# Cross-attention over 32 images: the last two groups of context products spread through the pipeline's fill

## The chip, the cores and the metric

One core of one Trainium2 chip. A core has five engines that run side by side, each with its own queue in program order: TensorE (PE: matmuls, with its weight loads PEld), VectorE (DVE), ScalarE (ACT), GpSimd (POOL) and SyncE (SP), which here only issues DMAs. They wait for one another by semaphores. The metric is the device time of one execution in microseconds (us), as the median of several.

## The reference

```python
q = heads(x @ to_q_w)                                  # x (32, 512, 640), 20 heads of 32
txt = ctx[:, :77]                                      # ctx (32, 77, 1024); the other three parts are empty
p = softmax(q @ heads(txt @ to_k_w).T / sqrt(32))
out = merge(p @ heads(txt @ to_v_w)) @ to_out_w + to_out_b + x
```

The context has 77 rows per image, so the three further attentions of the reference have no keys and add nothing. All is float32, and the kernel keeps that accuracy by splitting each matmul operand into a high and a low part and taking three products (high x high, high x low, low x high).

## The kernel before

**Context first.** The 32 x 77 = 2464 context rows are taken in five groups of up to 512 (`GROUPS_KV`; the last, `LAST` = 4, has 416). For each group the context is loaded (`load_context`), transposed on VectorE in eight pieces (`transpose_context`, line 164), split (`split_context`: high part on ScalarE, low part on VectorE), and multiplied by the key and the value weights: five chunks j of 128 channels, eight pieces k, three matmuls each (`context_product`, line 186). One such step of three matmuls is what the tables call a token. A finished key chunk is split and stored to `k_dram` (`split_keys`, two buffers `ks`), a finished value chunk is turned on VectorE, split and stored to `v_dram` (`split_values`, two buffers `vs`). The loops of lines 362 to 414 do this: the values of group g, with the next group's context in between, then the keys of group g + 1. The weights are split on the way in the first group (`first`, line 311). While group 3's values are made, x of image 0 is loaded by SP (line 391), then transposed on VectorE (line 404) and split, high part on ScalarE and low part on POOL. The keys of group 4 follow in two rounds. Only its values are left over.

**Attention by pairs.** Image b and chunk c of 128 channels (four heads) make a pair n = 5 b + c, 160 in all. A pair passes through these steps, spread over some five pairs' time: query product (15 matmuls, five tokens), its split (high on ScalarE, halves copied on POOL, low on VectorE), four score tiles (three matmuls each, into three PSUM banks), row maximum on VectorE, four exponentials per tile on ScalarE, sums, division on POOL, a block transpose on VectorE, a store to DRAM and a load back with keys on the partitions (`pd`, `raw`), a split of that (`pp`), six value matmuls (`pa`), the two halves added, a split (`at`), and, per image, 40 projection tokens (`po`) with output weights `wo_s`, residual and bias, and the store.

**The order is written out by hand.** A table of tokens gives the program order, and so each engine's queue: `FILL` (line 733) for images 0 and 1, `PLAN` (line 771) for each image from 2 to 30, and `LAST_` for the end. A token with a or b in front belongs to image 0 or 1, its digit is the chunk (b5 is chunk 0 of image 2, pair 10), and the letter is the step: q query, Q, k, g its split, s score tile, m maximum, e exponentials, r and N sums and division, z block transpose, w store, d load, c, R, l its split, v value product, A and a halves, h and L split, p projection, f, o, b output, T, X, x transpose and split of the next image's x, u the loads (uk keys, uv values, ux x, ur residual). Tokens with Y are special ones of the fill (`special`, line 900): YC value product of the last group, YT, YH, YL, YD its turning, split and store by POOL's queue, Yk key loads, Yx the load of image 1's x, Yq, YQ, Yc, Yg pair 0's query, Ym the memsets of `vb`, Yw the output weights, Yb the bias. Only the order inside one engine's queue counts; between engines the semaphores decide.

**Memory.** Buffers stand in pools that are opened and released at places in this order, and a tile in reused memory waits for the last use of what was there. Before the table starts, the pools of the context (`kvw`, `kvc`, `kvt`, and the eight banks `psk`) are released and `main` and `ps` opened; `open_late` (line 725) releases `kvp` and the three banks `psv` when the first rows are loaded (token a3d0), and the first Yw releases `kva`.

Of the kernel before, what the change touches and what calls it, by code (L numbers as in the profile page):

```python
# [24 lines left out]
Q = 32  # L25
# [26 lines left out]
def kernel(  # L52
# [83 lines left out]
    kvt = tc.alloc_tile_pool(name="kvt", bufs=2, side="right")  # L136
# [8 lines left out]
    wk_s = kvt.tile([P, NK, 2, C], FPR, name="wk_s", bufs=1)  # L145
    GROUPS_KV = [(g0, min(G, NT - g0)) for g0 in range(0, NT, G)]
    cts, pks, pvs, css, craws, wraws = ({} for _ in range(6))
# [16 lines left out]
    def transpose_context(g, k):  # L164
        gn = GROUPS_KV[g][1]
        craws[k] = kvt.tile([P, G], F32, tag="craw", name="craw")
        nc.vector.transpose(
            craws[k][:, :gn].rearrange("p (a j) -> p a j", j=Q),
            css[g][0][:, : gn // Q, k * Q : (k + 1) * Q],
        )  # L170

    def split_context(g, k):
        gn = GROUPS_KV[g][1]
        ct = kvp.tile([P, 2, G], FPR, tag="ct", name="ct", bufs=9)
        split(ct[:, 0, :gn], ct[:, 1, :gn], craws.pop(k)[:, :gn])
        cts[g, k] = ct
# [22 lines left out]
    def keys(g, j, k):  # L199
        context_product(pks, "pk", g, j, k, wk_s[:, :, :, j * P : (j + 1) * P], psk)  # L200
# [5 lines left out]

    def split_keys(g, j):
        g0, gn = GROUPS_KV[g]
        ks = kvt.tile([P, 2, G], FPR, tag="ks", name="ks")
        split(ks[:, 0, :gn], ks[:, 1, :gn], pks.pop(j)[:, :gn])  # L210
        engine = nc.gpsimd if g + 1 < len(GROUPS_KV) else nc.sync if j < 3 else nc.scalar
        j0 = GROUPS[GROUP_OF[j]][0]
        engine.dma_start(
            k_dram[GROUP_OF[j]][:, :, j - j0, g0 : g0 + gn].bitcast(F32), ks[:, :, :gn].bitcast(F32)
        )
# [6 lines left out]
    def value_parts(j):  # L222
        vs, na = vss[j % 2], GROUPS_KV[LAST][1] // Q
        return vs[:, :na, 0], vs[:, :na, 2], vs[:, :na, 2].bitcast(F32)

    def turn_values(j):
        na = GROUPS_KV[LAST][1] // Q
        nc.vector.transpose(
            value_parts(j)[2], pvs.pop(j)[:, : na * Q].rearrange("p (a d) -> p a d", d=HD)
        )  # L230

    def high_values(j):
        hi, lo, vt = value_parts(j)
        nc.scalar.copy(hi, vt)

    def low_values(j):
        hi, lo, vt = value_parts(j)
        nc.vector.tensor_tensor(lo, vt, hi.bitcast(F32), ALU.subtract)

    def store_values(j, i):  # L240
        g0, gn = GROUPS_KV[LAST]
        dst = v_dram[g0 : g0 + gn, :, j].rearrange("(a t) i c d -> i t a (c d)", t=Q)
        nc.gpsimd.dma_start(  # L243
# [4 lines left out]
    def split_values(g, j, between=None):  # L248

        g0, gn = GROUPS_KV[g]  # L250
        na = gn // Q
        vs = vss[j % 2]
        vt = vs[:, :na, 2].bitcast(F32)
        nc.vector.transpose(vt, pvs.pop(j)[:, :gn].rearrange("p (a d) -> p a d", d=HD))
        if between is not None:
            between()
        split(vs[:, :na, 0], vs[:, :na, 2], vt)
        dst = v_dram[g0 : g0 + gn, :, j].rearrange("(a t) i c d -> i t a (c d)", t=Q)
        for i in range(HPC):
            nc.sync.dma_start(  # L260
                dst[i].bitcast(F32),
                vs[i * Q : (i + 1) * Q, :na].rearrange("p a c d -> p a (c d)").bitcast(F32),
            )

    xts, xss, xpool = {}, {}, []

    def load_x(b, quarters=range(4)):
# [5 lines left out]
        for q in quarters:  # L273
            nc.sync.dma_start(xs[q * Q : (q + 1) * Q, :, :], src[q])
# [10 lines left out]
    def high_x(b, c, high=nc.scalar.copy):  # L285
        xts[b, c] = xpool[0].tile([P, 2, S], FPR, tag="xt", name="xt", bufs=7)
# [18 lines left out]
    zero = kvt.tile([P, 2, G], FPR, name="zero", tag="ks")[:, 0]  # L305
# [5 lines left out]
    def first(*ks):  # L311
# [3 lines left out]
        for k in ks:  # L315
            split_context(0, k)
            split_weights(wk_s[:, k], wk, k)
# [44 lines left out]
    for g in range(LAST):  # L362
        for j in range(NC_):
# [13 lines left out]
            if j == NC_ - 1:  # L377
# [3 lines left out]
                split_values(g, 3, (None, split_wq, split_wo, None)[g])  # L381
                context(g + 1, *range(3, NK))
                if g + 1 == LAST:
                    kvw.release()
                    kvc.release()
# [639 lines left out]
```

## Time and profile before

| | |
|---|---|
| median of the runs | 1873.78 us (1872.28 to 1873.96) |
| profiled execution | 1872.94 us, its span 1871.1 us |
| TensorE busy, weight loads | 1852.1 us, 1660.1 us |
| VectorE, ScalarE, POOL busy | 1559.3, 1525.0, 1298.7 us |
| values of group 3 start | 200.4 us |
| keys of group 4 start | 227.6 us |
| `FILL` starts | 250.0 us |
| first score tile of pair 0, 5, 10 | 265.6, 310.0, 360.5 us |

A row of a stretch of the span gives each engine's busy time in it with its number of instructions, the clock granted to TensorE as a share of full speed, the busy share of the DMA engines, and GB/s. A row of a group gives line, engine, operation, the tiles, the count, busy us and mean ns of one, and the idle time before it with what ended it. In a row in order of time the first number is the start, the second the length, and a bracket says how long the engine had been idle and what released it.

### The profile page before, as it was taken

To read this page: it belongs to the slowest core of one execution; us is meant where nothing else is said; L and a number is where in the kernel's file an instruction comes from. 1 tells how busy PE (TensorE), PEld (TensorE's weight loads), DVE (VectorE), ACT (ScalarE), POOL (GpSimd) and SP (SyncE) were. 2 spreads that over 40 slices of the span, in tenths; PEclk is the share of its full clock that TensorE was granted. 3 is DMA by queue.
4 is the path that set the end of the run, shared out by engine and by line. 5 is a ranking of instruction groups with operands and counts; after the bars stand their busy time and mean duration, and the time that the engine had idled before them with its cause. 6 is when DMAs were issued, how large, how long until landed. Compare 5 with 4: busy or idle time off the path is not lost.

```text
span 1871.1 us, 37477 instructions
## 1 busy us (share of the span) xinstructions
PE 1852.1 (99%) x10332; PEld 1660.1 (89%) x10332; DVE 1559.3 (83%) x2494; ACT 1525.0 (82%) x6210; POOL 1298.7 (69%) x1116
## 2 busy tenths in 40 slices
PE   9999998999999999999999999999999999999998
PEld 7888897899999999999999999999999999999998
DVE  5445347999999999999999999999999999999996
ACT  3233228999999999999999999999999999999984
POOL 1100057888877877777787778877788778877774
PEclk9999999999999999999999999999999999999999
DMA  9878879999998999999899999999989989999985
GB/s 183 200 196 245 199 166 254 233 245 238 242 239 234 240 232 237 238 231 245 237 238 238 237 242 238 238 233 236 241 232 245 240 236 240 229 241 236 238 222 185
DMA packets 565023, 431.37 MB, mean 231 GB/s; under 512 B 191120, under 2 KB 473168, under 8 KB 564816
## 3 DMA queue, kind: packets, MB, share of 16 engines
q1 hardware_dynamic: 559760, 413.62, 86.6%
q0 software_dynamic: 4416, 14.34, 2.3%
q8 instruction: 85, 1.39, 0.3%
q14 instruction: 122, 1.00, 0.2%
q10 hardware_dynamic: 640, 1.02, 0.2%
HBM read 247.17 MB, written 181.64 MB: 229 GB/s over the span
## 4 chain that ended last, share of the span: by engine, by line
PE 81%; ACT 1%; DVE 1%; DMA 1%; issue 0%; POOL 0%; SPq 0%; DVEq 0%; POOLq 0%; ACTq 0%
PE po L685 30%; PE pq L481 28%; PE pa L632 12%; PE sc L516 11%; ACT pn L541 1%; DMA pd<-z 0%; DMA raw<-pd 0%; DVE qt L723 0%; ACT pp L601 0%; DVE z L562 0%; SPq L571 0%; DVE xs L278 0%; POOL v_dram L243 0%; PE pv L191 0%; DVE nm L527 0%
## 5 line engine op out<-in xcount | busy, mean ns | idle before, releaser
L541 ACT ACTIVATE pn<-sc,nm 128x77 f32<-128x77 f32 x2560 | 795.7, 342 | 37.3 <-DVE nm L527 33.8
L685 PE MATMUL po<-wo_s,at 128*128 128x320 f32 x3840 | 710.8, 311 | 0.4 <-DVE at L667 0.2
L685 PEld LDWEIGHTS po<-wo_s,at 128*128 128x128 f32 x3840 | 620.7, 189 | 42.9 <-DVE xr L700 0.6
L481 PE MATMUL pq<-xt,wq_s 128*128 128x512 f32 x2400 | 599.1, 395 | 4.5 <-DVE qt L723 4.5
L541 ACT ACTIVATION_READ_ACCUMULATOR pn<-sc,nm 128x1 f32 x2560 | 567.1, 222 | 0.0
L481 PEld LDWEIGHTS pq<-xt,wq_s 128*128 128x128 f32 x2400 | 436.8, 188 | 86.2 <-ACT pn L541 3.9
L556 POOL TENSOR_TENSOR pn<-pn,rs 128x1232 f32<-128x1232 f32 x160 | 387.0, 2419 | 88.9 <-DVE rs L551 87.0
L632 PE MATMUL pa<-pp,vb 128*128 128x512 f32 x960 | 343.1, 406 | 2.9 <-DVE at L667 1.4
L516 PEld LDWEIGHTS sc<-kb,qt 128*128 128x128 f32 x1920 | 305.4, 189 | 20.7 <-ACT pn L541 6.1
L527 DVE TENSOR_REDUCE nm<-sc 128x4 f32<-128x308 f32 x640 | 294.9, 466 | 22.8 <-PE sc L516 17.1
L516 PE MATMUL sc<-kb,qt 128*128 128x154 f32 (+1 forms) x1920 | 304.2, 275 | 3.8 <-ACT pn L541 2.6
L719 POOL CAST qt<-qt 64x512 fp32r<-64x512 f32 x320 | 195.1, 610 | 139.0 <-ACT qt L715 122.2
L650 DVE TENSOR_TENSOR pa<-pa,aw 64x512 f32<-64x512 f32 x320 | 222.2, 694 | 51.4 <-ACT aw L646 44.2
L617 POOL TENSOR_TENSOR pp<-raw,pp 64x512 fp32r<-64x512 f32 x160 | 206.2, 1289 | 73.2 <-ACT pp L599 58.2
L562 DVE STREAM_TRANSPOSE z<-pn 128x1280 f32<-128x1280 f32 x160 | 241.1, 1507 | 6.1 <-POOL pn L556 2.4
L646 ACT COPY aw<-pa 64x1024 f32<-64x1024 f32 x160 | 161.9, 1012 | 91.9 <-PE pa L632 91.0
L723 DVE TENSOR_TENSOR qt<-pq,qt 64x512 fp32r<-64x512 f32 x320 | 216.8, 677 | 17.6 <-ACT qt L715 12.9
L292 POOL TENSOR_TENSOR xt<-xs,xt 128x512 fp32r<-128x512 f32 x160 | 204.0, 1302 | 35.8 <-ACT xt L288 30.9
L678 POOL TENSOR_TENSOR xr<-xr,bias 128x640 f32<-128x640 f32 x128 | 204.2, 1596 | 12.7 <-issue 2.8
L610 DVE TENSOR_TENSOR pp<-raw,pp 128x1024 fp32r<-128x1024 f32 x160 | 194.3, 1214 | 0.0
L632 PEld LDWEIGHTS pa<-pp,vb 128*128 128x128 f32 x960 | 174.4, 190 | 13.0 <-DVE pp L610 1.6
L601 ACT CAST pp<-raw 128x1024 fp32r<-128x1024 f32 x160 | 168.0, 1050 | 0.8 <-DMA v_dram<-vs 0.8
(48 smaller groups left out, 1577.7 us busy)
## 6 DMA issues: line engine op xcount, KB each, us to landing
pd<-z SPq DMA_DIRECT2D x640, 160.0 KB, 3.5
raw<-pd SPq DMA_DIRECT2D x160, 512.0 KB, 4.4
xs<-in_x_dram SPq DMA_DIRECT2D x128, 320.0 KB, 5.7
xr<-in_x_dram SPq DMA_DIRECT2D x128, 320.0 KB, 3.9
out_dram<-xr SPq DMA_DIRECT2D x127, 320.0 KB, 3.8
raw<-pd SPq DMA_DIRECT2D x160, 128.0 KB, 3.9
v_dram<-vs SPq DMA_DIRECT2D x80, 192.0 KB, 4.1
k_dram<-ks POOLq DMA_DIRECT2D x20, 512.0 KB, 4.3
```

The source lines that it names most:

```text
L481: nc.tensor.matmul(pqs[n], wq_s[:, k, a, j * P : (j + 1) * P], xts[b, k][:, c, :], start=(k == 0 and m == 0), stop=(k == NC_ - 1 and m == 2),)
L516: nc.tensor.matmul(sc[:, cols], qt[:, m, t * P : (t + 1) * P], keys_, start=(m == 0), stop=(m == 2),)
L527: nc.vector.tensor_reduce(nm, sc[:, :KCOLS].rearrange("p (h k) -> p h k", k=NKEY), AX.X, ALU.max, negate=True)
L541: nc.scalar.activation(pnb[n % 2][:, at, :NKEY], sc[:, i * NKEY : (i + 1) * NKEY], AF.Exp, bias=nm[:, i : i + 1], accum_out=sms[n][:, at : ...
L556: nc.gpsimd.tensor_tensor(pf, pf, rs.unsqueeze(2).to_broadcast([P, NQ * HPC, NKEY]), ALU.mult)
L562: nc.vector.transpose(z.rearrange("p b t j -> p t b j"), pn.rearrange("p (t h) k -> p t (h k)", t=NQ).rearrange("p t (b i) -> p t b i", i=Q),)
L617: nc.gpsimd.tensor_tensor(pp[64:, 4, :], raw[:64, 2, :], pp[:64, 4, :].bitcast(F32), ALU.subtract)
L632: nc.tensor.matmul(pas[n][:, p, :], vb[:, p, t, :], pp[:, c, :], start=(c == p), stop=(c == p + 2),)
L650: nc.vector.tensor_tensor(pa[64 * p : 64 * p + 64, 0], pa[:64, p], aw[:, p], ALU.add)
L678: nc.gpsimd.tensor_tensor(xrs[b, t], xrs[b, t], bias, ALU.add)
L685: nc.tensor.matmul(pos[b, t, h][:, :HALF], ats[b * NC_ + j][:, a, t * P : (t + 1) * P], wos[0][:, j, c, h * HALF : (h + 1) * HALF], start= ...
L723: nc.vector.tensor_tensor(qt[rows, 1 + w, :], pqs[n][rows], qt[rows, 0, :].bitcast(F32), ALU.subtract)
```

## The change

- `FILL` begins one group earlier. The values of group 3 (YV, turned Yt, split Yh and Yl, stored Ys by SP), the context of group 4 (Yr transpose, Yf high, Yd low part), x of image 0 (Yz load by POOL's queue, Ya transpose, YU high, Yu low part), the keys of group 4 (YJ, split YI and Yi, stored Yo by SP) and its values (YC) are tokens of one table now. The loops end with group 2's values and group 3's keys. All 160 pairs have the same steps as before; `PLAN` and `LAST_` are as they were.
- The last YC stands at pair 5 (between b0R and b0h), where it stood at the end of pair 2 (before a3s0).
- The key weights `wk_s` are two tiles (384 and 256 columns) in two pools, each split by its own instructions.
- The buffers of the attention are opened in five steps: `open_small` (kb0 and the small tiles, where the context was), `open_first` (qt, pn, over the first key weights), `open_second` (kb1, z, vb, over the second), `open_values` (raw, pp, aw, one at, over the first value weights) and `open_late` (the other at, bias, xr, wo_s, over the rest). The banks are opened by `open_banks` at the first YJ: four for scores and query, two and two for the context products. The memsets of kb and pn are tokens (Yn, Yp).
- The split parts of x stand in two pools of 4 and 3, and the eight `at` buffers are fixed tiles used in turn.

```diff
-    wk_s = kvt.tile([P, NK, 2, C], FPR, name="wk_s", bufs=1)
+    wk_s = [
+        pool.tile([P, NK, 2, c1 - c0], FPR, name=f"wk_s{i}")
+        for i, (pool, (c0, c1)) in enumerate(zip((kvt, kvu), WV))
+    ]
...
-            split_weights(wk_s[:, k], wk, k)
+            part = wraws.pop((id(wk), k))
+            for (c0, c1), dst in zip(WV, wk_s):
+                split(dst[:, k, 0], dst[:, k, 1], part[:, c0:c1])
...
-    for g in range(LAST):
+    for g in range(LAST - 1):
...
-                    load_x(0)
...
-    for i in range(NQ):
-        transpose_x(0, i)
-    for c in range(NC_):
-        split_x(0, c)
-
-    for round_ in (range(3), range(3, NC_)):
-        for k in range(NK):
-            for j in round_:
-                keys(LAST, j, k)
-        for j in round_:
-            split_keys(LAST, j)
...
+    def open_banks():
+        nonlocal ps, psa, psb
+        if ps is None:
+            psk.release()
+            ps = ctx.enter_context(
+                tc.tile_pool(name="ps", bufs=1, space=PSUM, side="right", reuse_waits="tile")
+            )
+            psb = tc.alloc_tile_pool(name="psb", bufs=2, space=PSUM, side="right", reuse_waits="tile")
+            psa = tc.alloc_tile_pool(name="psa", bufs=2, space=PSUM, reuse_waits="tile")
...
+    def open_first():
+        if not qts:
+            open_small()
+            kvt.release()
+            pool = ctx.enter_context(tc.tile_pool(name="first", bufs=1, reuse_waits="tile"))
+            qts.extend(pool.tile([P, 3, S], FPR, name=f"qt{n}") for n in range(2))
+            pnb.extend(pool.tile([P, NQ * HPC, KPAD], F32, name=f"pn{n}") for n in range(2))
...
+        "YV00 YV10 YV20 YV11 YV30 YV31 YV01 YV12 YV02 YV13 YV32 YV03 YV04 YV05 YV14 Yr0 YV06 Yf0 Yz1 Yd0 "
+        "YV07 Yz2 YV15 Yt0 YV40 Yz0 Yr1 Yz3 YV21 Yr2 Yf1 YV41 Yh0 YV42 Yf2 YV33 Yd2 Yr3 YV22 Yl0 YV23 "
+        "Yf3 Yd1 Ys00 YV16 Yr4 Ys01 YV24 Ya1 Ys02 YV43 Ya2 YV34 Ys03 Yf4 Yd3 YV35 Yr5 Yd4 YV25 Ya3 YV17 "
+        "YV44 Yt1 YV26 Ya0 Yf5 YV36 YU0 YV27 Yh1 YV45 YU1 Yt2 YV46 YU2 Yd5 YU3 Yl1 YV37 Yu2 Yr6 Yh2 Ys11 "
+        "YV47 Yf6 Yl2 Ys13 Yu1 Yr7 Ys10 Yd6 Yf7 Ys21 Ys22 Ys23 Ys12 Yt3 Yd7 YU4 Yu4 Yu3 Yu0 Yx0 Ys20 Yx2 "
+        "Yx1 Yh3 Yn0 Yt4 YJ00 YJ01 YJ20 YJ21 YJ10 YJ02 YJ22 YJ30 YJ11 YJ03 YJ12 YJ13 YJ23 YJ14 YJ24 YJ15 "
+        "YJ04 YJ05 YJ06 YJ16 YJ25 YJ31 YJ07 YJ32 YI0 YJ17 Yi0 Yq0 Yl3 YI1 Yo0 Yh4 YJ26 Yi1 YJ40 Yl4 Yo1 "
+        "YJ27 Yx3 YJ41 Yq1 YI2 Yq2 Yi2 YJ42 Yo2 Yq3 Ys41 YJ33 Ys43 Yq4 a1T1 YJ43 Ys30 YQ YJ44 Yg1 Yc1 "
+        "Yk030 YJ45 Yg0 Yc0 Yk000 YJ34 Yk020 a0T0 YJ46 Yp1 Yk010 YJ35 Yk031 YJ36 Yk001 Yp0 Yk021 YJ37 "
+        "Yk011 YJ47 YI3 a0K00 YC00 Yi3 YI4 a0K01 a0q0 Yi4 Yo3 a0q1 Yo4 Yn1 YC01 Ys40 Ym0 a0s0 a0q2 Ys42 "
...
+        "b2g1 b2A b2uv05 b2s3 b3uk011 b2m2 b3q0 b3c0 b2uv01 b2m3 b2a0 b2e1 b3q1 b2uv02 b2k0 b2a1 b3q2 "
+        "b3d1 b1K10 b2e2 b2uv06 b2z b2b0 b3s0 b3uk031 b3q3 b3h b3q4 b3L b3l Yw3 b3c1 b3p1 b3m0 b2w1 b3p4 "
...
+        elif op == "V":
+            values_of_chunk(LAST - 1, *arg, psk)
...
+        elif op == "z":
+            load_x(0, arg, nc.gpsimd)
...
+        elif op == "J":
+            open_banks()
+            keys(LAST, *arg, bank_of("k", arg[0]))
```

300 lines of the change are left out of this document (185 added, 115 removed), and 66 rows, old and new, of the table FILL.

## The prediction

> **What bounds the kernel now.** I read the page's engine lines first, then the stretches of the span by stage, then TensorE's waits and its order of time where it waits.
>
> ```profile
> PE 1852.1 (99%) x10332; PEld 1660.1 (89%) x10332; DVE 1559.3 (83%) x2494; ACT 1525.0 (82%) x6210; POOL 1298.7 (69%) x1116
> ```
>
> ```profile
> 0.00:8.10 8.10, 4.65 (x13) 3.39 (x13) 1.86 (x4) 2.53 (x3) 6.96 (x14) 1.00 0.95 139
> 8.10:200.40 192.30, 192.30 (x841) 158.68 (x842) 91.74 (x144) 58.69 (x101) 11.37 (x17) 0.99 0.90 210
> 200.40:265.60 65.20, 64.09 (x311) 57.74 (x310) 24.80 (x40) 14.77 (x27) 19.31 (x21) 1.00 0.66 166
> 265.60:310.00 44.40, 41.62 (x220) 36.96 (x218) 30.25 (x51) 32.08 (x162) 34.60 (x41) 1.00 0.91 238
> 310.00:360.50 50.50, 44.19 (x208) 35.41 (x208) 45.27 (x71) 48.13 (x197) 38.69 (x32) 0.93 0.94 248
> 360.50:1800.00 1439.50, 1439.50 (x8343) 1307.11 (x8342) 1315.20 (x2110) 1326.77 (x5577) 1148.50 (x965) 1.00 0.91 237
> 1800.00:1871.10 71.10, 65.79 (x404) 60.79 (x403) 50.20 (x78) 42.08 (x148) 39.27 (x29) 1.00 0.67 204
> ```
>
> The columns are window, length, then busy us of PE, PEld, DVE, ACT and POOL, the granted clock, DMA share, GB/s. From 360.5 to 1800 TensorE never idles: nothing can be won there without less work, and the change leaves that table alone. TensorE idles 3.45 us at the start, 5.3 in the drain, and 1.1 + 2.8 + 6.3 = 10.2 in the three rows from 200.4 to 360.5: there the pipeline fills. In 310:360.5 ScalarE is busy 48.13 of 50.5 us and VectorE 45.27; TensorE has too little to do and waits for them.
>
> ```profile
> PE pq L481 <- DVE qt L723: 4.5, 3, 2.1
> PE sc L516 <- ACT pn L541: 2.6, 3, 2.0
> PE pk L191 <- ACT wk_s L103: 2.0, 1, 2.0
> ```
>
> ```profile
> 320.00:322.00 2.00, 0.33 (x3) 0.33 (x3) 1.86 (x3) 1.98 (x11) 0.42 (x1) 1.00 1.04 238
> 322.00:324.00 2.00, 1.16 (x5) 0.53 (x3) 1.88 (x3) 2.00 (x13) 1.27 (x1) 0.60 0.79 293
> 324.00:326.00 2.00, 2.00 (x8) 1.76 (x9) 2.00 (x4) 2.00 (x14) 0.44 (x1) 0.50 0.95 280
> ```
>
> The waits are for query parts and for score banks. After the 2.0 us wait the granted clock fell to half; the 0.93 of row 310:360.5 is 0.07 x 50.5 = 3.5 us of clock lost.
>
> **The idea in numbers.** Matmul work is conserved, so the change is worth what the fill loses less what the new fill loses. I find where pair 10 (b5), from which TensorE waits no more, makes its first score tile. Today's marks, pairs 0, 3, 5 and 10:
>
> ```profile
> 265.57 0.68 PE L516 MATMUL sc<-kb,qt 128*128 128x308 f32 x3
> 296.90 0.86 PE L516 MATMUL sc<-kb,qt 128*128 128x308 f32 x6
> 310.03 0.60 PE L516 MATMUL sc<-kb,qt 128*128 128x308 f32 x3
> 360.50 0.49 PE L516 MATMUL sc<-kb,qt 128*128 128x308 f32 x3
> ```
>
> Prices for a token: V and the 416-wide J and C from the first two rows below (27.36/40 = 0.684; 14.72/26 = 0.566), q 3.49/5 = 0.70, s 0.69/2 = 0.345, v 0.47/2 = 0.235, p 2.24/5 = 0.45, one e on ScalarE 1.23.
>
> ```profile
> 200.37 27.36 PE L191 MATMUL pv<-ct,wv_s 128*128 128x512 f32 x120
> 227.56 14.72 PE L191 MATMUL pk<-ct,wk_s 128*128 128x416 f32 x78
> 379.05 3.49 PE pq L481 x15
> 378.36 0.69 PE sc L516 x6
> 386.22 0.47 PE pa L632 x2
> 383.31 2.24 PE po L685 x15
> 322.59 1.23 ACT pn L541 x8
> ```
>
> **Key weights in two tiles.** Eight casts of 640 columns become 384 and 256, on ScalarE and VectorE each.
>
> ```profile
> L103 ACT CAST wk_s<-wraw 128x640 fp32r<-128x640 f32 x8 | 5.8, 725 | 3.4 <-DMA wraw<-in_L_xattn_to_k_w_dram 3.4
> L103 ACT CAST wv_s<-wraw 128x384 fp32r<-128x384 f32 x8 | 4.1, 511 | 9.7 <-DMA wraw<-in_L_xattn_to_v_w_dram 9.7
> L103 ACT CAST wv_s<-wraw 128x256 fp32r<-128x256 f32 x8 | 3.2, 401 | 0.0
> ```
>
> The first key matmul waited 2.0 us for that cast; the first piece is 0.21 shorter: -0.2 us (0 if its data decide). The cost, 0.511 + 0.401 - 0.725 = 0.19 us for each of eight steps, lies on an engine busy 58.69 of 192.3 us, and matmuls there never wait: nothing.
>
> **Values of group 3, then its followers (V, r/f/d, x).** V starts at 200.4 as before: everything ahead is the same. Until pair 0's first score the table holds 40 V (27.4), 40 J (22.6), 7 q (4.9) and 2 C (1.1): 56.0 us, so 256.4 without waits. The same count on today's kernel, from 227.56: 40 keys, 13 C, 10 q make 37.0, plus the 1.1 us wait that 200.4:265.6 shows (65.2 less 64.09): 265.7 against 265.57 measured. The attention thus starts 9 us sooner and leaves 38 C steps for later instead of 27.
>
> What must be in time here is on the queues. VectorE is held by the last key split of group 3 until 211.5, 11.1 us into V, and then has 27 transposes and differences of 0.6 to 0.8 us:
>
> ```profile
> 210.82 0.69 DVE L104 TENSOR_TENSOR ks<-pk,ks 128x512 fp32r<-128x512 f32 x1 [2.89 <-ACT ks L103]
> 243.42 6.30 POOL L292 TENSOR_TENSOR xt<-xs,xt 128x512 fp32r<-128x512 f32 x5 [30.93 <-ACT xt L288]
> L167 DVE STREAM_TRANSPOSE craw<-cs 128x416 f32<-128x416 f32 x8 | 4.6, 598 | 0.1
> L278 DVE STREAM_TRANSPOSE xs<-xs 128x640 f32<-128x640 f32 x128 | 104.8, 821 | 7.3 <-DMA xs<-in_x_dram 7.3
> v_dram<-vs SPq DMA_DIRECT2D x20, 192.0 KB, 3.7
> xs<-in_x_dram SPq DMA_DIRECT2D x12, 320.0 KB, 5.8
> k_dram<-ks SPq DMA_DIRECT2D x3, 416.0 KB, 3.4
> kb<-k_dram SPq DMA_DIRECT2D x24, 28.9 KB, 2.6
> k_dram<-ks POOLq DMA_DIRECT2D x20, 512.0 KB, 4.3
> 252.92 8.07 SPq L451 DMA_DIRECT2D kb<-k_dram  x12
> ```
>
> In us from V's start: x leaves by POOL's queue, four issues from +12, and lands (5.8) by about +21. VectorE's list, in its order, then puts x's transposes at +24 and the last context transpose at +29, after which ScalarE makes the last high part of x (YU4), near +30. POOL's last low part (u0) is three of 6.30/5 = 1.26 later, +34. SP has the next batch's x (Yx0) waiting for u0, and behind it the store Ys20; this lands near +39 at 3.7, +42 if it stands behind x. The transpose Yt4 waits for it on VectorE, and behind it stand Yi0, Yl3, Yi1. By the order in which banks come free, Yq0 takes the bank Yt4 empties: due at +41.3; YJ40 needs Yi0's bank at +42.6. So 0 to 2 us of wait; I take 0.7. Next, Yo2 (about +46) lands 3.4 later, and the eight loads behind it take 8.07/12 = 0.67 each and a landing of 2.6: +57, where pair 0's score is due at +56.7: 0 to 2, I take 0.8. The memsets of POOL (kb, pn, vb) are the old ones, moved. The last three (Yn1, Ym0, Ym1) wait for the last J at +53.6 and a key store, and stand on POOL ahead of pair 1's query copies; at about 1.26 us each, the price of a low part of x, the nearest row, they end near +58, while pair 1's query is ready near +60 behind ScalarE's second e: nothing, and 2 us if the key store lands late. The other openings wait for steps long done: the raw tile for YC27, some 3 us of TensorE ahead of its load a3d0, the last buffers for YC47 and the value stores, a pair ahead of their first use. The fixed at tiles and the two pools for x keep the old rotation of 8 and 7: nothing, since TensorE idles nowhere in the part where they rotate, with the same reuse distance as before. The four loads of x leave SP and cost POOL issue time while it only waits; the two key stores of ScalarE's queue go to SP, behind nothing but Yx3. Range of this stage 0 to 4 us; sum: 256.4 - 0.2 + 1.5 = 257.7.
>
> **Pairs 0 to 4.** Between their first score tile and pair 5's the table has 37 C, 23 q, 20 s and 6 v: 20.9 + 16.1 + 6.9 + 1.4 = 45.3; ScalarE has 20 e; today's row 265.6:310, with 19 e, keeps it busy 32.08 us. TensorE binds. Interleaving costs something: today's pairs 0 to 2 count 30.4 and take 31.3 (265.57 to 296.90), so 46.6. Value loads stand on SP behind stores (YD), and a query bank behind VectorE (today 1.1 us): 1.3 (0 to 3). Pair 5 at 305.6, against 310.03.
>
> **Pairs 5 to 9.** Here before and after differ little. TensorE: 29 q, 20 s, 30 v, 13 p, 1 C, in all 40.6, against 24, 20, 33, 14 and none, 37.7 today. ScalarE loses against today one e (1.23), one A and two c1 (1.05 each by the first row below, all 1024 wide) and a c0, and gains a Q and an H of about the size of a c0: some 3.9 less, 44.3. VectorE loses one z (1.51), and two a against a T and an L: 43.7.
>
> ```profile
> L601 ACT CAST pp<-raw 128x1024 fp32r<-128x1024 f32 x160 | 168.0, 1050 | 0.8 <-DMA v_dram<-vs 0.8
> L562 DVE STREAM_TRANSPOSE z<-pn 128x1280 f32<-128x1280 f32 x160 | 241.1, 1507 | 6.1 <-POOL pn L556 2.4
> ```
>
> So they remain the bound over TensorE. Today's stage has them at 48.13/50.5 = 95% and 45.27/50.5 = 90%: 46.6 or 48.6. I take 47.5. Low end 40.6 (all hidden), high end today's 50.5. The output weights (Yw) now load one pair ahead of their use instead of five; they are taken to lie in this range. Pair 10 at 353.1, and 0.4 us more work after it: 353.5 against 360.5, a gain of 7.0.
>
> [...] Row 310:360.5 has loads at 35.41 against 1307.11/1439.5 = 91% in the steady part, so 11.5 us lost, not the 6.3 of idle; the trace's count (50.5 - 37.7 = 12.8) agrees. By busy time alone the gain could not exceed 10.2 in the whole fill; by loads about 15.
>
> **Sum.** The span 1871.1 less 7.0 is 1864.1; the profiled execution's 1872.94 becomes 1865.9; the median shown, 1873.78, is 0.84 above that execution: 1866.8.
>
> **Rivals.**
> 1. *TensorE alone binds the fill.* All waits hidden: pair 10 at 256.2 + 45.3 + 40.6 = 342.1, some 18 us gained, 1855; with half of the waits left, 1861. Against: both helpers have over 43 us to do in those 40.6.
> 2. *ScalarE sets the end anyway.* The exponentials are as many, and ScalarE stays at its pace: pairs 5 to 9 take 50.5 and pairs 0 to 4 wait 3: gain about 2, 1872. For: its 95% today.
> 3. *A wait in front halves the clock.* If Yq0 or pair 0's keys are 2 us later than I took, the rows at 322 repeat themselves where TensorE binds: 2 + 3.5 us, 1872. [...]
> 4. *Slower: SP's queue order.* Yt4 hangs on Ys20, that on Yx0, that on u0, that on x coming by POOL's queue. Each us that x is late beyond its slack of 1 us is a us of TensorE at Yq0. It decides from about 11 us: 7 to eat the gain, 3.7 to be seen; 1878. For: one chain through four queues. Against: POOL's queue today lands 512 KB in 4.3 us (k_dram<-ks).
> 5. *The spreading does nothing*: the context steps fill TensorE where ScalarE is not the bound; that is rival 2 with 2 us less, and it is counted there.
>
> **How the numbers follow.** A measurement of this kernel tells about 0.2%, 3.7 us, from no change. Forecast 0.58 (1863 to 1870), rival 1 0.12, rivals 2 and 3 together 0.17, rival 4 0.13. Faster 0.70, same 0.17, slower 0.13. The range 1860 to 1874 leaves out about half of rival 1 and rival 4.
>
> **What the next profile would show.** Right: TensorE's idle between 250 and 350 down from 10.2 to some 5 us, pair 0's first score near 258, pair 10's near 353, ScalarE busy over 90% in pairs 5 to 9, clock never at 0.5. Wrong: pq or pk waiting for vs or ks near 240; the score tile at 257 waiting for kb; matmuls of po waiting for wo_s; idle in the steady part.

## The result, and the profile after

The changed kernel takes 1861.16 us (median of six runs, 1859.27 to 1864.14) against 1873.87 (six runs, 1872.28 to 1875.28) of the kernel before on the same chip: ratio 0.9935, 95% interval 0.9923 to 0.9948, a gain of 12.7 us. The forecast was 1866.8 in a range of 1860 to 1874. The profiled execution took 1860.52 us with a span of 1858.7; before it was 1872.94 and 1871.1.

The engine line of the profile after:

```profile
PE 1843.8 (99%) x10332; PEld 1656.9 (89%) x10332; DVE 1563.8 (84%) x2502; ACT 1524.9 (82%) x6218; POOL 1301.7 (70%) x1120
```

TensorE is still busy 99% of the span. To see where the 12.4 us of span went, both spans are cut at the same marks: the first score tile of pairs 0, 5, 10 and 15, and the very last score tile. The columns are those of the prediction's rows: window, length, busy us of PE, PEld, DVE, ACT and POOL, granted clock, DMA share, GB/s. The kernel before (pairs 0 to 4, pairs 10 to 14, pair 15 to the last score tile, the rest; pairs 5 to 9 are the prediction's row 310.00:360.50):

```profile
265.57:310.03 44.46, 41.68 (x221) 36.99 (x219) 30.28 (x52) 32.11 (x162) 34.60 (x41) 1.00 0.91 238
...
360.50:410.81 50.31, 50.31 (x292) 45.66 (x291) 46.25 (x74) 47.12 (x204) 41.16 (x35) 1.00 0.95 246
410.81:1830.29 1419.48, 1419.48 (x8238) 1289.50 (x8237) 1296.15 (x2079) 1305.97 (x5480) 1130.19 (x949) 1.00 0.91 237
...
1830.29:1871.10 40.81, 35.50 (x221) 32.73 (x219) 23.01 (x36) 15.75 (x40) 16.42 (x11) 1.00 0.55 178
```

The changed kernel from the values of group 3 (which start at 200.52) on:

```profile
200.52:257.00 56.48, 56.18 (x268) 49.68 (x266) 26.45 (x42) 14.41 (x27) 18.15 (x20) 1.00 0.69 177
257.00:303.78 46.78, 46.09 (x247) 42.49 (x247) 32.80 (x51) 35.52 (x174) 38.32 (x40) 1.00 0.88 217
303.78:352.19 48.41, 43.12 (x220) 35.29 (x220) 42.60 (x69) 44.35 (x190) 40.39 (x38) 1.00 0.88 264
...
352.19:404.30 52.11, 51.40 (x296) 46.05 (x294) 48.20 (x74) 47.42 (x200) 39.79 (x35) 1.00 0.90 256
404.30:1818.83 1414.53, 1414.51 (x8237) 1288.14 (x8236) 1296.69 (x2079) 1305.50 (x5480) 1130.48 (x949) 1.00 0.89 238
...
1818.83:1858.70 39.87, 35.48 (x221) 32.71 (x219) 23.04 (x36) 15.77 (x40) 16.45 (x11) 1.00 0.56 185
```

| stage, us | before | forecast | after |
|---|---|---|---|
| up to pair 0's first score tile | 265.57 | 257.7 | 257.00 |
| pairs 0 to 4 | 44.46 | 47.9 | 46.78 |
| pairs 5 to 9 | 50.47 | 47.5 | 48.41 |
| pairs 10 to 14 | 50.31 | 0.4 more | 52.11 |
| pair 15 to the last score tile | 1419.48 | as before | 1414.53 |
| the rest | 40.81 | as before | 39.87 |

Pair 10 starts 8.3 us sooner (forecast: 7.4, with 0.4 of more work behind it), pairs 10 to 14 give 1.8 of that back, and with pair 15, at 404.30 against 410.81, the fill has gained 6.5 us where 7.0 was forecast. The other 5.9 us, 4.95 of them in the steady part, come from where the table is the same word for word. That is the first thing to explain; the second is what sets the pace of pairs 5 to 9, where TensorE still idles 48.41 less 43.12, 5.3 us.

TensorE's waits of over 0.5 us in the order of time, from the values of group 3 to pair 10 (start, length, what it did, in brackets the idle time before it and what ended it):

```profile
286.29 0.34 PE L577 MATMUL sc<-kb,qt 128*128 128x154 f32 x1 [0.69 <-POOL qt L783]
312.77 0.73 PE L577 MATMUL sc<-kb,qt 128*128 128x308 f32 x3 [1.90 <-ACT pn L602]
318.25 0.47 PE L694 MATMUL pa<-pp,vb 128*128 128x512 f32 x1 [0.89 <-DVE at L731]
321.37 2.31 PE L542 MATMUL pq<-xt,wq_s 128*128 128x512 f32 x9 [0.81 <-DVE qt L787]
344.66 0.47 PE L694 MATMUL pa<-pp,vb 128*128 128x512 f32 x1 [1.16 <-ACT pp L663]
```

The two waits feared in front (pair 0's first query product at 242.41, its first score tile at 257.00) are not there. The longest is again one for a score bank, at 312.77, with 1.90 us about as long as the 1.96 us one of before; but this time the clock stayed at 1.00. The signs that the prediction had named for being right came: between 250 and 350 us TensorE idled 5.98 us instead of 10.21, ScalarE was 92% busy in pairs 5 to 9, and the clock never fell in the fill. Of its signs of being wrong only a little is there, the idle 0.71 us in pairs 10 to 14 (`378.67`, for VectorE's at part).

### The profile page after: what moved, and what is told of

It is laid out like the page before. It is cut to its first block, busy times and chain, and to the rows that moved or that the text cites. A ratio compares the mean times of both kernels' runs of the same rounds, so it can differ in the third digit from the quotient of the medians.

```text
span 1858.7 us, 37494 instructions
## 1 busy us (share of the span) xinstructions
PE 1843.8 (99%) x10332; PEld 1656.9 (89%) x10332; DVE 1563.8 (84%) x2502; ACT 1524.9 (82%) x6218; POOL 1301.7 (70%) x1120
## 4 chain that ended last, share of the span: by engine, by line
PE 93%; ACT 2%; DMA 1%; DVE 1%; SPq 1%; issue 1%; POOL 0%; DVEq 0%; ACTq 0%; POOLq 0%
PE po L750 30%; PE pq L542 28%; PE pa L694 12%; PE sc L577 11%; PE pk L204 6%; PE pv L204 6%; ACT pn L602 1%; DMA pd<-z 1%; SPq L531 0%; SPq L633 0%; DVE z L624 0%; POOL xt L320 0%; DMA v_dram<-vs 0%; DVE pp L672 0%; DMA cs<-in_ctx_dram 0%
```

## The experiments

Each kernel was profiled once. A single profile's marks move between executions: over nine kernels with the changed front, pair 0 started between 254.25 and 257.00. So lengths of stages are compared, and times where there are several runs.

**Is it the spreading, or the earlier start?** The attention starts 9 us sooner, and 38 steps of YC are spread over pairs 0 to 5. The first kernel keeps the start and takes back a part of the spreading:

```diff
-"... YC26 YC27 a3q0 ... a3Q YC30 ... YC32 ... YC40 ... YC46 ... b0R YD31 YC47 b0h ..."
+"... YC26 YC27 YC30 YC31 ... YC37 YC40 YC41 ... YC47 a3q0 ... a3Q ... b0R YD31 b0h ..."
```

> The changed kernel with the sixteen YC steps of chunks 3 and 4 moved up to stand right behind YC27, ahead of pair 3's first score tile (the value turns, splits and stores stay where they are). Nine us of TensorE work (16 x 0.566) thus leave pairs 3 to 5 and delay pair 3. Theory A, spreading is what gains: pair 3's first score tile comes 9.1 later (294.3 against 285.2), ScalarE and VectorE (60.1 and 58.4 us busy between pair 3 and pair 10) then bind the rest, TensorE idles 9 us or so more, pair 10 starts at about 357 to 359 instead of 352.2, the time is 1866 to 1869, and the clock may fall to half again. Theory B, starting the attention 9 us sooner is what gains and the place of the filling steps is indifferent: pair 10 within 1 us of 352.2 and the time within 2 us of 1861.

Measured: 1869.44 us (ten runs, 1866.55 to 1871.34), ratio to before 0.9978 (0.9969 to 0.9988): against its own runs of the kernel before, 1873.06, a gain of 3.6 us is left of the 12.7. The profiled execution was one of the slowest of the ten (1871.26). Pair 3 started at 293.19, pair 5 at 311.17 and pair 10 at 364.40. Rows of that kernel: pairs 3 and 4, pairs 5 to 9, and one stretch of 3.42 us with the one behind it:

```profile
293.19:311.17 17.98, 12.65 (x52) 10.38 (x51) 11.44 (x19) 13.90 (x60) 14.08 (x15) 0.81 0.67 155
311.17:364.40 53.23, 47.28 (x216) 38.33 (x217) 45.59 (x71) 46.39 (x200) 42.12 (x40) 0.90 0.79 236
308.76:312.18 3.42, 0.54 (x3) 0.37 (x3) 2.79 (x5) 3.40 (x19) 2.14 (x3) 1.00 0.88 228
312.18:315.59 3.41, 3.34 (x9) 2.26 (x9) 2.83 (x4) 2.26 (x12) 2.27 (x4) 0.50 0.59 145
```

Pairs 3 and 4 lost 15 of the 16 moved steps, about 8.5 us of TensorE's work, and took 17.98 us, as the changed kernel does with that work (285.23 to 303.78 is 18.55): TensorE simply idled, 5.3 us, and ran partly at half clock. Pair 10 came 3.9 us later than in the kernel before, although the attention had started at 255.99, 9.6 us sooner; that this execution is still ahead of the kernel before it owes to what stands behind the fill, above all the steady part (1465.09 us from pair 10 to the last score tile against 1469.79). So theory A holds, with pair 10 later than its 357 to 359. A part of that is the clock: it stood at half for 17.1 us between 298.5 and 336.1, against 6.8 us in the kernel before. In this table the earlier start is worth nothing without work for TensorE to do meanwhile.

**Was the half clock a cost of its own?** The second kernel is the one before, with something to do in its 2.0 us wait (YE0 takes a spare bank, YE4 puts four matmuls into it):

```diff
-"... b0A b3p0 ... b1q4 b1c1 ..."
+"... b0A YE0 b3p0 ... b1q4 YE4 b1c1 ..."
```

> The kernel before, with four idle matmuls (128x512, about 0.23 us each, into a spare bank that nobody reads) put into the 2.0 us wait at 319.7, ahead of pair 6's first score tile. Theory A, the half clock is a cost of its own: it follows TensorE being busy only 39% of the stretch 318.98 to 322.40; with 0.93 us more in it the clock stays at 1.00 and pair 10 starts 3.5 us sooner, at 357.0, time 1870.4. Theory B, ScalarE and VectorE set the end of that stretch anyway: the clock stays at 1.00 but pair 10 stays within 0.7 us of 360.5 and the time within 1 us of 1873.9. Theory C, the clock falls for another reason: it still shows 0.50 near 322 to 329.

Measured: 1873.37 us (ten runs) against 1873.06 (19 runs), ratio 1.0001 (0.9992 to 1.0010). Rows of that kernel: pairs 5 to 9, and three stretches in a row:

```profile
310.60:360.55 49.95, 43.80 (x213) 35.16 (x213) 45.32 (x71) 48.16 (x197) 38.73 (x32) 0.97 0.95 249
319.49:322.91 3.42, 2.32 (x11) 1.51 (x9) 2.92 (x5) 3.39 (x12) 1.50 (x1) 1.00 0.95 253
322.91:326.32 3.41, 1.98 (x9) 1.40 (x10) 3.41 (x6) 3.41 (x21) 1.45 (x2) 1.00 0.80 294
326.32:329.74 3.42, 3.42 (x12) 2.96 (x12) 3.10 (x6) 3.17 (x17) 3.30 (x3) 0.50 0.97 252
```

The half clock fell from 6.83 to 3.42 us and the stage from 50.47 to 49.95; the time did not move. None of the three theories came in full: behind the filled stretch the clock stayed at 1.00, as in A and B, the next stretch (1.98 us of work) was followed by half clock, near where C has it, and the time is B's. That TensorE would have waited there anyway, so that a slow clock costs nothing, fits this but is not shown: the interval does not exclude a gain of up to 1.5 us. The half clock is not always free. The changed kernel, 256 bytes further on in memory and otherwise the same, shows that:

```diff
+    const.tile([P, 64], F32, name="pad")
     wq_s = const.tile([P, NC_, 2, C], FPR, name="wq_s")
```

> The changed kernel with 256 bytes per partition left empty ahead of wq_s, so that the tiles on that side of the memory all lie 256 bytes further; no instruction differs. From pair 10's first score tile to the last score tile the changed kernel took 1466.8 us against 1470.0 before, though the table of that part is the same. Theory A, the addresses make that difference: it moves by more than 1 us here. Theory B, it is set by the order of work and repeats: 1466.8 within 0.5 us, time within 1.5 us of 1861. Theory C, it differs from execution to execution: it lies anywhere between 1465 and 1471 though nothing else changed.

Measured: 1861.94 us (four runs, 1861.26 to 1863.66), and 1465.60 us from pair 10 to the last score tile. That is 1.04 less than in the changed kernel, but 0.94 of it lie in pairs 10 to 14; from pair 15 on it is 1414.43 against 1414.53. So a shift of all addresses together does nothing (theory B, once the first pairs are left out). But its profiled execution had two stretches at half clock where the changed kernel's had none. Rows: pairs 5 to 9, the two stretches ahead of a drop, and the one behind the first:

```profile
303.36:354.98 51.62, 45.86 (x220) 37.91 (x220) 44.49 (x69) 44.47 (x190) 40.69 (x38) 0.93 0.82 243
309.82:313.23 3.41, 1.59 (x11) 1.22 (x10) 3.06 (x5) 3.37 (x15) 3.26 (x5) 1.00 0.99 383
313.23:316.65 3.42, 3.42 (x11) 2.85 (x10) 3.35 (x7) 3.42 (x17) 3.19 (x4) 0.50 0.85 309
320.06:323.47 3.41, 1.70 (x8) 1.41 (x9) 3.38 (x6) 2.16 (x6) 3.19 (x3) 1.00 0.98 380
```

The same instructions took 51.62 us there instead of 48.41. The wait for the score bank was no longer (1.82 us), but it fell into one stretch of 3.41 us, while in the changed kernel's execution it began 1.9 us into a stretch:

```profile
309.00:312.41 3.41, 1.86 (x12) 1.49 (x10) 3.19 (x8) 3.36 (x15) 3.32 (x6) 1.00 0.84 294
312.41:315.83 3.42, 3.06 (x16) 2.58 (x17) 3.35 (x5) 3.42 (x19) 3.27 (x3) 1.00 1.00 376
```

So 3.2 us between two executions of one order of work, in step with the clock: 2.7 us of it are TensorE's longer busy time, the rest longer waits. That the spread of the changed kernel's runs (1859.27 to 1864.14) is of this kind is likely and not shown, as single stretches are known of the profiled execution alone. Each run's mean granted clock points the same way: 0.998 in the two longest (1863.75 and 1864.14), 0.999 in the other four, where one stretch of 3.41 us at half lowers the mean by 0.0009.

**What sets the pace of pairs 5 to 9?** The prediction said ScalarE and VectorE. Two kernels take work off one of them, leaving a part of the computation out:

```diff
+        if 5 <= n < 10 and t % 2:          # in exps: one instruction instead of four
+            nc.scalar.activation(pnb[n % 2][:, at : at + HPC, :NKEY], sc[:, :KCOLS]..., AF.Exp, bias=nm[:, 0:1])
+            nc.scalar.copy(sms[n][:, at : at + HPC], nm)
+            return
```

```diff
+        if 5 <= n < 10:                    # in block_transpose
+            return
```

> The changed kernel, but in pairs 5 to 9 the exponentials of score tiles 1 and 3 are one instruction over all four heads, with one head's maximum and without sums (their place is filled from the maxima): some 0.6 us off ScalarE for each of ten tiles, 6 us of the 44.4 it is busy from pair 5 to pair 10. The softmax of image 1 is thereby left out in part. Theory A, ScalarE sets the pace of pairs 5 to 9: the 48.4 us from pair 5 to pair 10 fall by 4 to 6, to 42.5 to 44.5, and the time to about 1856. Theory B, VectorE (42.6 us busy there) and the chain of waits through it set it: they stay above 47.

> The changed kernel without the block transposes of pairs 5 to 9 (the stores send what stood in z before): 5 x 1.5 = 7.5 us off VectorE's 42.6 between pair 5 and pair 10. The transposition of image 1's attention weights is left out. Theory A, ScalarE sets the pace there: the 48.4 us stay within 1.5. Theory B, VectorE does: they fall by 4 or more, to 44 or less. If both this and the kernel with fewer exponentials gain some 2 us, neither alone is the bound, and what is lost are waits from one to the other.

> The changed kernel with both cuts in pairs 5 to 9: two score tiles of four with one exponential instruction for all heads (6 us less on ScalarE), and no block transposes (7.5 us less on VectorE); image 1's softmax and transposition are left out in part. Alone, the first left pair 5 to pair 10 at 48.35 us (with one stretch of 3.41 us at half clock) and the second at 51.48 (two such stretches), against 48.41 in the changed kernel (none) and 51.62 in the same program 256 bytes further on (two). Theory A, ScalarE and VectorE bind together, and what one gains the other takes: with both cut it falls to 45 or less (TensorE's count is 40.6), up to 47 if a half-clock stretch falls into it. Theory B, the waits come from the chains through POOL and the DMAs (query copies, keys, rows loaded back), which both cuts leave as they are: 47.5 or more, with TensorE's waits for POOL, for DMAs and for the query parts as before.

Measured: 1860.1 us (two runs), 1861.29 (three) and 1857.5 (two). The row of pairs 5 to 9 of each, in this order:

```profile
302.47:350.82 48.35, 44.25 (x221) 36.62 (x220) 43.03 (x69) 39.56 (x137) 41.69 (x38) 0.96 0.90 265
303.69:355.17 51.48, 45.99 (x220) 37.67 (x220) 40.43 (x65) 44.47 (x190) 40.25 (x38) 0.93 0.84 244
```

```profile
300.80:349.37 48.57, 43.92 (x221) 36.42 (x221) 39.73 (x65) 39.25 (x137) 41.22 (x38) 0.96 0.90 262
```

ScalarE's 44.35 us fell to 39.56 and the stage stayed. VectorE's fell to 40.43 from the 44.49 of the padded kernel, which also had two stretches at half clock, and the stage was as long as there (51.48 and 51.62). With both at 39 to 40 of 48.57 us it stayed again. If a stretch at half clock is put at 1.6 us (3.2 for two, above), the three would have been 46.7, 48.3 and 47.0 without one: 1.7 us at most for 4 to 8 us of work. Over the stage as a whole neither engine's sum is the bound, nor the two together; theory B of the last run holds, though its waits are not the same ones as before. POOL and the DMAs were not made lighter in any kernel. What TensorE waited for in that kernel, from 250 to 352 us:

```profile
PE sc L577 <- ACT pn L612: 2.2, 1, 2.2
PE po L762 <- DMA wo_s<-wo_dram: 1.9, 2, 1.4
PE pq L542 <- DVE qt L799: 1.0, 2, 0.6
```

The first is the wait at 312.77 again, and ScalarE did not cause it by being full: it idled ahead of it, in the changed kernel too (ScalarE's own rows there):

```profile
306.86 0.54 ACT L262 CAST vs<-vs 128x416 fp32r<-128x416 f32 x1 [1.64 <-DVE vs L256]
308.51 0.33 ACT L602 ACTIVATE pn<-sc,nm 128x77 f32<-128x77 f32 x1 [1.11 <-DVE nm L588]
```

The first of these waits for the last value turn YT4 on VectorE, the second for the maximum of pair 5, which stands behind YT4; the exponential that would free a bank comes behind that. YT4 itself waited only 0.23 us for its store to land. It was late because VectorE was full (VectorE's row of YT4, then the stretch from pair 5's first score tile to the wait in the changed kernel, and the same stretch in the kernel with both cuts):

```profile
306.17 0.62 DVE L256 STREAM_TRANSPOSE vs<-pv 128x416 f32<-128x416 f32 x1 [0.23 <-DMA v_dram<-vs]
303.78:312.77 8.99, 7.09 (x38) 5.88 (x37) 8.55 (x15) 6.19 (x28) 6.28 (x10) 1.00 0.88 266
...
300.80:311.00 10.20, 8.01 (x43) 6.72 (x43) 9.62 (x17) 7.14 (x31) 7.17 (x11) 1.00 0.96 270
```

VectorE is 95% and 94% busy in these 9 to 10 us: the first block transpose that was left out, pair 5's, starts only at 323.43 in the changed kernel, so leaving them out took nothing off VectorE here. For this first part of the stage VectorE's sum as the bound is not refuted by these kernels; only the order of its work is tried below. The new waits for the output weights (wo_s) are what the prediction had named as a risk.

**Can the chain be cut?** Three orders of the table, each adding to the one before:

```diff
-"... b0s0 b0uk120 b0R YD31 YC47 b0h b0q0 ... b0L b0q1 YD32 YT4 ... YH4 b0s1 YL4 b0q3 b0m0 YD40 b2T3 b0e0 ... b0m1 ..."
+"... b0s0 b0m0 b0uk120 b0R YD31 YC47 b0h b0e0 b0q0 ... b0L b0s1 b0q1 YD32 b0m1 YT4 ... YH4 YL4 b0q3 YD40 b2T3 ..."
```

```diff
-"... YH4 YL4 b0q3 ... b0Q b0v3 ... b0s2 b0A b0s3 b0k1 b0m2 ... b0e2 YD30 ... b0T0 b0e1 b1q0 ..."
+"... YH4 b0e1 YL4 b0s2 b0m2 b0q3 ... b0Q b0e2 b0v3 ... b0A b0s3 b0k1 ... YD30 ... b0T0 b1q0 ..."
```

```diff
-"... b1l b0z b1q2 ... b1q3 b0w0 b1m0 b2x0 b1c1 b0w2 b1m1 b1L b0w3 ..."
+"... b1l b1q2 ... b1q3 b1m0 b2x0 b1c1 b1m1 b1L b0z b0w0 b0w2 b0w3 ..."
```

> The changed kernel with the first maxima of pair 5 taken ahead of the last value turn: b0m0 right behind b0s0, b0e0 behind b0h, b0s1 ahead of b0q1, b0m1 ahead of YT4. In the changed kernel ScalarE idles 1.64 + 1.11 = 2.75 us from 305.2 to 308.5 because the first maximum of pair 5 stands on VectorE behind YT4, which waits for a store to land, and TensorE then waits 1.9 us at 312.8 for a score bank. Theory A, ScalarE binds pairs 5 to 9 and that gap is lost for good: pair 10 starts 1.5 to 2.75 us sooner, near 350, time 1858.5 to 1859.7. Theory B, VectorE binds as much (94% busy from 300 to 326): moving its work only changes the order, pair 10 within 0.7 us of 352.2, time within 1 us of 1861.

> The kernel with pair 5's first maxima taken sooner, and its exponentials too: b0e1 behind YH4 and b0e2 behind b0Q instead of behind b0A and b1c0, b0s2 and b0m2 ahead of b0q3. With the maxima alone the wait at 312 stayed (1.82 us), because ScalarE had b0Q, b0A and b0e2 in front of b0e1, whose score bank b1s0 wants. Theory A, the wait is one of ScalarE's order: it goes, the stretch of 3.41 us around 311 is busy over 0.55, the clock stays at 1.00 there, and pair 5 to pair 10 takes 46 to 47.5 us (48.4 and 48.8 so far), time 1858 to 1859.5. Theory B, ScalarE's and VectorE's sums leave no room: another wait of 1 to 2 us comes in its place before 325, pair 5 to pair 10 stays within 48 to 49, time 1860 to 1861.5.

> The last kernel, and the block transpose of pair 5's predecessor (b0z, 1.5 us of VectorE) behind the maxima and the at part that TensorE waits for next (b1m0, b1m1, b1L), its stores with it. Theory A: the 0.8 us wait near 321 and the 0.9 near 318 go as well, pair 5 to pair 10 takes 45 to 46.5 us, time 1857 to 1858.5. Theory B: the later turn is missed two pairs on (its stores and the rows loaded back), waits for rows appear near 340, and nothing is won over the last kernel.

Measured: 1860.81 us (four runs, 1858.00 to 1861.53), 1859.28 (four, 1857.96 to 1860.98; ratio to before 0.9920, 0.9906 to 0.9935) and 1861.07 (four, 1859.94 to 1862.76). Pairs 5 to 9 took 48.84, 48.12 and 50.40 us in the profiles, with one, no and one stretch at half clock. The maxima alone left the wait (1.82 us), as the exponentials stood behind other work of ScalarE. With the exponentials moved it went, and two others were there, on POOL's query copies and VectorE's at part:

```profile
313.79 0.45 PE L577 MATMUL sc<-kb,qt 128*128 128x154 f32 x2 [1.58 <-POOL qt L783]
319.81 0.47 PE L694 MATMUL pa<-pp,vb 128*128 128x512 f32 x1 [1.70 <-DVE at L731]
```

The first is theory B. In the second the wait of 1.82 us went and the clock stayed, and the time lies in theory A's range, but the stage lies in theory B's, with other waits in place of the old. The third won nothing over the second, as theory B has it. In all three a wait removed is followed by one elsewhere. The second of these kernels has the lowest median of all that compute the whole result, but its interval overlaps the changed kernel's; it isn't shown to be better.

**Where do the 5 us behind pair 15 come from?** The table there is the same, TensorE never waits, the clock is 1.00. The distance from a score tile to the same tile one image later (285 matmuls), read from the trace, is 49.180 us in the kernel before and 48.993 us in the changed one, equal to a ns or two from image to image, but for two images of the changed kernel (49.01 and 49.11); 28 images at that difference would be 5.2 us; 4.95 were measured. There are three variants of the kernel before. The first two take over traits of the changed one; the third puts the same tiles at other places:

```diff
-tc.tile_pool(name="ps", bufs=1, space=PSUM, reuse_waits="tile")
+tc.tile_pool(name="ps", bufs=1, space=PSUM, side="right", reuse_waits="tile")   # and psv on the other side
```

```diff
-            at = late[0].tile([P, 2, S], FPR, tag="at", name="at", bufs=8)
+            at = held[n % 8]               # eight fixed tiles; and wk_s in two tiles, as in the change
```

```diff
-    bias, kb0, kb1, pn0, pn1, qt0, qt1, z, vb0, vb1    # order in which main's tiles are made
+    vb0, vb1, z, qt0, qt1, pn0, pn1, kb0, kb1, bias
```

> The kernel before, with the two groups of PSUM banks on opposite sides (the four of scores and query where the changed kernel has them). From pair 10's first score tile to the last, kernels with the old layout took 1469.8 and 1470.1 us, kernels with the new one 1466.6, 1465.1, 1465.7 and 1465.6, although the table there is the same and TensorE never waits. Theory A, it is the place of the banks: 1465 to 1467 here. Theory B, it isn't: 1469.5 to 1470.5.

> The kernel before with two of the change's parts alone, which act at different places: the key weights in two tiles, and the eight at buffers as fixed tiles used in turn. Key weights: the first key matmul starts 0.2 us sooner by the prediction (today it waits 2.0 us for the cast of the first piece); if its data decide, 0; the values of group 3 start at 200.4 within the 1 us by which executions differ. At buffers: if they make the 3 to 5 us by which the unchanged part of the table became shorter, pair 10 to the last score tile takes 1465 to 1467 here; if not, 1469.5 to 1470.5.

> The kernel before with the tiles of its main pool opened in the reverse order (values, z, query parts, pn, keys, bias), so that the same buffers lie at other addresses. One image of the steady part takes 49.18 us in four kernels of the old layout and 48.99 in six of the new one, equal to a ns within each, so the program sets it; banks and the at tiles don't. Theory A, the addresses of these buffers against each other do: the image takes something else here, and pair 10 to the last score tile differs from 1469.8 to 1470.1 by 1 us or more. Theory B, they don't: 49.18 and 1469.5 to 1470.5.

Measured (one run each): 1871.91, 1874.15 and 1874.01 us. The rows from pair 15's first score tile to the last, with the banks exchanged and with fixed at tiles, and from pair 10's with the tiles in reverse order:

```profile
409.31:1828.88 1419.57, 1419.57 (x8237) 1289.50 (x8236) 1297.02 (x2079) 1307.22 (x5480) 1130.66 (x949) 1.00 0.91 237
```

```profile
410.52:1830.34 1419.82, 1419.82 (x8238) 1289.51 (x8236) 1296.65 (x2079) 1306.75 (x5480) 1130.56 (x949) 1.00 0.90 237
```

```profile
366.25:1831.70 1465.45, 1465.45 (x8528) 1334.09 (x8526) 1342.63 (x2153) 1354.48 (x5684) 1172.98 (x982) 1.00 0.90 238
```

Banks and at tiles do nothing: 49.180 us an image. With the tiles in reverse order the image takes 49.033 us and the part from pair 10 on is 4.3 us shorter than in the kernel before (1465.45 against 50.31 + 1419.48), where the change itself brought 3.2 (52.11 + 1414.53). That is theory A, the addresses. But it is one kernel, and its fill differs too (other memsets wait for other steps, pair 10 starts at 366.25), so a rival is left: the state in which the fill hands over to the steady part.

The traces speak against this rival. The 285 steps of an image, from the start of one matmul to the start of the next, repeat to 2 ns, in images that nothing holds up, in all nine kernels with the new buffers, whatever their pair 10 (349.4 to 364.4), and also in the four kernels with the old fill and the old order of buffers. Between the two groups about a hundred of the 285 steps differ, by 13 ns at most, so no single wait makes the 0.187 us. The kernel without turns in pairs 5 to 9, which has the new buffers, seems to run one image in the old rhythm (two images in a row of it, from one score tile to the same one an image later):

```profile
455.39:504.57 49.18, 49.18 (x288) 44.57 (x286) 45.35 (x73) 45.66 (x192) 39.52 (x34) 1.00 0.91 243
504.57:553.56 48.99, 48.99 (x287) 44.60 (x286) 44.92 (x72) 45.27 (x191) 39.24 (x34) 1.00 0.93 251
```

Taken apart by tiles, it does not. The rows are the query products (pq) of an image of the kernel before and of that image of 49.18, then the value products (pa) of that image and of the next one; the first busy time is TensorE's:

```profile
410.81:459.99 49.18, 18.57 (x75) 13.67 (x75) 6.77 (x10) 2.97 (x5) 1.00 0.92 233
...
455.39:504.57 49.18, 18.48 (x75) 13.67 (x75) 6.77 (x10) 3.02 (x5) 1.00 0.91 243
...
455.39:504.57 49.18, 10.96 (x30) 5.50 (x30) 10.36 (x15) 8.41 (x11) 1.00 0.91 243
504.57:553.56 48.99, 10.79 (x30) 5.45 (x30) 10.39 (x15) 8.00 (x11) 1.00 0.93 251
```

Its query products take the 18.48 us of the new rhythm. Only two value matmuls, at 479.76 and 480.07, are 0.08 and 0.10 us longer than an image later; that the sum is 49.18 again is chance.

So what is shown: the same steady table has at least three rhythms, 49.180, 49.033 and 48.993 us an image; each program keeps one of them and comes back to it when an image was held up; and neither the banks nor the at tiles nor a common shift of all addresses choose. That the places of main's buffers against each other choose is the likelier account, and it rests on one kernel; why a place should cost some ns at a hundred matmuls is open.

The key weights: in the kernel with them in two tiles the first key matmul started at 7.82 us after a wait of 1.86, against 8.09 and 2.00 before and 8.28 and 2.07 in the changed kernel. The 0.2 us is lost in what executions differ by anyway.

## Why the prediction was right, and where it was off

The sign, the range and the mechanism in the fill held (TensorE does context products where it used to wait), and the fill's size within half a us. That closeness is partly luck: the errors of its stages, -0.7, -1.1, +0.9 and +1.4 us, nearly cancel. The whole gain was 5.6 us larger than forecast, as it came in part from where the prediction had put nothing. By its own steps:

- *Front, 257.7.* Measured 257.00: of the "0 to 2 us of wait; I take 0.7" for the chain Yt4, Ys20, Yx0, u0, and of the 0.8 for pair 0's keys, nothing came. The chain was as tight as computed, though. VectorE's row of Yt4, and TensorE's of pair 0's query product, which takes that bank and was due at 241.8 by the working:

```profile
241.64 0.72 DVE L256 STREAM_TRANSPOSE vs<-pv 128x512 f32<-128x512 f32 x1 [2.26 <-DMA v_dram<-vs]
```

```profile
242.41 0.97 PE L542 MATMUL pq<-xt,wq_s 128*128 128x512 f32 x3
```

- *Pairs 0 to 4, 47.9.* Measured 46.78 with 0.69 us of idle instead of 1.3; the 3% for interleaving held (46.09 busy against 45.3 counted is 1.7%).
- *Pairs 5 to 9, 47.5.* Measured 48.41, near in size, but for the wrong reason. The step that failed is "So they remain the bound over TensorE": a busy share of 95% and 90% was read as a bound of the whole stage, and taking 4 to 5 us off the one, the other or both changed the stage by less than 2. Most of the stage is TensorE's own 43.12 us (40.6 counted, so interleaving cost 6% here, against the 3% seen in pairs 0 to 2), and 5.3 us are waits in chains through VectorE, ScalarE and POOL. Only in its first 9 us, where VectorE is 95% busy, may the step hold.
- *Clock.* "3.5 us of clock lost" in the kernel before: giving half of it back gained 0.5 us in the stage and nothing clear of noise in the time. So the third rival's price was probably too high for that place; for the changed kernel it is about right (1.6 us per stretch, estimated from the two executions above).
- *Behind pair 10.* "0.4 us more work" was 1.8: 0.5 us of it is one more projection step (TensorE's po 23.13 us instead of 22.64), and 0.71 is one idle time, as the waits of the fill ran on for another image; the rest is spread. "Nothing can be won there without less work", and of the moved buffers "nothing, since TensorE idles nowhere in the part where they rotate": this is the other step that failed. It measured 4.95 us from pair 15 on. The drain's 0.9 is less than what kernels with the same drain differ by (39.9 to 42.2).
- *The sum.* Fill 6.5 for 7.0, steady part 4.95 for 0, drain 0.9 for 0: 12.4 for 7.0 in the span. Without the change of rhythm, the forecast would have been about 1 us off; the mechanism it argued from earned about half of the gain.
- *Rivals.* TensorE alone (1855): no, the waits stayed. Its other price, 1861 with half of the waits left, is the time measured, but by chance: it takes the whole gain from the fill, which gave 6.5 us. ScalarE sets the end (1872): no, and it does not even set the stage. Slower by SP's queue order: its chain was there and had no slack to spare, but cost nothing. "The spreading does nothing": refuted, taking a part of it back leaves 3.6 us of the 12.7.
- *Weighing loads against busy time.* By the count of weight loads (the author's estimate) some 15 us could be won in the fill, by busy time at most 10.2. The fill gave 6.5, inside both, so this case doesn't decide. By occupancy ScalarE comes first in pairs 5 to 9 (92%), and taking 4.8 us off ScalarE moved the stage by 1.7 us at most.

## What to carry to other kernels

In a pipeline's fill, give TensorE independent work in the very slots where it would wait; starting a stage 9.6 us sooner without that gained nothing here. A helper that is busy 95% of a stage is a suspect and no more: take work off it before planning around it. Cut two traces at the same marks before explaining a difference: a few tenths of a per cent can come from a part whose program did not change (here 4.95 of 1871.1 us).

## What the runs showed of the hardware that was not expected

- *Half clock came in stretches of 3.41 us.* All times at half clock in the profiles were 3.41 or 6.83 us long (in the kernel before 8.37 to 11.79 and 322.40 to 329.23, in the changed one 8.63 to 12.04), but for the last one of each, which the end of the execution cuts off, and in one execution (the bunched kernel) they began at 298.5, 312.2, 322.4 and 332.7, whole multiples of 3.41 apart. Stretches at full clock with 0.54, 1.32, 1.59, 1.62 and 1.70 us of TensorE's work, in the fills of five kernels, were each followed by one at 0.50; after 1.86 us (the changed kernel) the clock stayed, and after 1.98 (the kernel before with its wait filled) it fell, so busy time isn't exactly what counts. The row of the kernel before, ahead of its drop at 322.4:

```profile
318.98:322.40 3.42, 1.32 (x7) 0.68 (x5) 2.93 (x5) 3.40 (x12) 1.44 (x1) 1.00 0.98 239
322.40:325.81 3.41, 2.71 (x8) 1.99 (x9) 3.41 (x6) 3.41 (x21) 1.52 (x2) 0.50 0.93 307
```

  None of these stretches was idle throughout. The one shown had 1.32 us of TensorE's work in 3.42, and its longest gap was 1.96 us.
- *Nearly the same wait went with half clock in one execution and not in another.* The same score tile waited 1.82 us in the padded kernel, all of it within one stretch of 3.41 us (1.59 us of work), and the next stretch was at 0.50; it waited 1.90 us in the changed kernel, from 1.9 us into a stretch on (1.86 us of work), and the next was at 1.00. That the place of the wait among these stretches decides fits both, and rests on them.
- *The steady part had more than one rhythm.* The same 285 matmuls took 49.180, 49.033 or 48.993 us, by program, each equal to a few ns over dozens of images; from pair 15 to the last score tile TensorE idled 0.02 us at most in 1414 to 1419. Between the first of these and the last about a hundred of the 285 differ, by 13 ns at most; no run here shows what makes the 0.4%.
